# Splitting the second layer's expert routing of a batch into two planned threads, with two buffers for the normed rows

## The chip, the cores and the metric

The kernel runs on one core of a Trainium2 chip. The metric is the device time of one execution in microseconds (us); less is better. The program is one launch; its five engines are TensorE (PE, matmuls and transposes), VectorE (DVE), ScalarE (ACT), GpSimd (POOL, which here also issues the indirect DMAs), and SyncE (SP, which issues most other DMAs). Each works through its own queue in order.

## The reference

Four layers, each an attention block and then a feed-forward block, work on `x` of 4 batches x 512 tokens x 128 numbers; a context of 154 tokens is used by the cross attentions. The change lies in the feed-forward block of the second layer (`L1_ffn`), a mixture of 8 experts with a fixed capacity. What it computes, cut:

```python
S = Bb * Tt                              # 2048 tokens
C = int(CAP_FACTOR * S / E)              # 320 places per expert
logits = xf @ gate_w + gate_b            # xf: the layer-normed x
probs = jax.nn.softmax(logits, axis=1)
topk_p, topk_i = jax.lax.top_k(probs, 2)
topk_pn = topk_p / jnp.sum(topk_p, axis=1, keepdims=True)
mask = jnp.zeros((S, E), bool).at[rows[:, None], topk_i].set(True)
rank = jnp.cumsum(mask.astype(jnp.int32), axis=0)       # over all tokens, in order
slot = jnp.where(mask & (rank <= C), rank - 1, C)
...
xin = x_pad[idx]                         # the rows of each expert's tokens
h = jax.nn.relu(jnp.einsum('ecd,edh->ech', xin, w1) + b1[:, None, :])
out = jnp.einsum('ech,ehd->ecd', h, w2) + b2[:, None, :]
```

A token's rank at an expert counts the tokens of earlier batches too, so batch b's ranks need the masks of batches 0 to b. An expert can only be computed when the rows of all batches are in place.

## The kernel before

Tokens lie on the 128 partitions, four tiles of 128 to a batch. `xs[b]` holds a batch's `x` in SBUF throughout. Layers one and two are run by one call of `run(units, threads)`, a planner that writes out the order of every engine's instructions by hand. A *unit* is a quarter of a batch's attention (four of the sixteen heads): scores (`L906` in the second layer), row maxima (`L912`), their transpose (`L678`, copied to `nmT` at `L680`), the scores again with the maxima subtracted (`L927`, `L933`; the last 26 context tokens at `L945`, `L951`), exponentials on ACT (`L937`, `L954`), sums (`L779`, `L786`, kept by `L972`/`L974`), and products with the values (`L980`, `L987`, copied out at `L992`). There are 32 units, and they are the frame.

Everything else is a *thread*: a Python generator that stops at each `yield` with a text such as `"P.3 V1.3"`, the cost in us that the planner is to assume on PE (P), DVE (V), ACT (A), GpSimd (G) or DMA (D) for the next step. A thread is given with its total of PE work, the unit at which it may start, the unit by which it is due, and the threads that must be over before it starts. The planner keeps an estimated clock of each engine and puts steps of the threads into the gaps of the units, by due time, if the engine would be free. The engines then follow that order; only the semaphore waits between them are found by the framework. So the cost texts and due times decide what stands behind what in each queue. They do not change what an instruction costs.

The threads of batch b in the second layer are:

- `l1_in(b)`: norm of `xs[b]` into `xi`, its transpose, and the values.
- `qk64`: queries (`L1083`, copied by ACT at `L1086`) and keys (`L1098`, `L1103`) of a unit.
- `l1_end(b)`: reciprocals of the sums on DVE (`L1427`), their spread over partitions (`L1433`), the division (`L1440`), the output projection (`L1445`, added at `L1449`), and the bias on POOL (`L1451`).
- `l1_to(b)`: the routing. Norm: `bn_stats` and `bn_aggr` on DVE (`L240`, `L241`), `rstd` on POOL (`L268`, `L269`), the application `xr` (`L260`, on POOL, for the last batch on DVE); transpose (`L308`, copied by ACT at `L314`) and logits (`L401`, `L406`); softmax (`L1463` to `L1470`, its exponential on ACT at `L1465`); two rounds of `top2` (`L351` to `L358`, `L1475`); the sum of the two best `den` and the mask (`L1479` to `L1482`); ranks (`ranks`: running counts on DVE at `L1157`, matmuls at `L1155` and `L1158`); limits (`L1486`, `L1489`); and for each of the two choices the picks (`L1164` to `L1504`, eleven instructions) and four indirect DMAs on POOL that scatter the rows `xr` to the experts' places (`L1175`), each followed by a tiny memset.

`l1_to(b)` starts when `l1_end(b)` and `l1_to(b - 1)` are over. Its tile `xr` has one buffer, so `xr` of a batch can be written only after the scatters of the batch before have read theirs:

```python
xn = yield from norm2(rt, "xr", xs[b], fast=b == B - 1)
```

After `run`, POOL loads the experts' biases (`L1531`), SP loads expert weights (`L1536`, `L1538`) and, once all scatters have landed, the gathered rows of each expert (`L1541`); the experts' matmuls follow on PE, and then the layers three and four. A further thread, `turned_weights`, prepares weights of later layers in the meantime and ends with eight large DMAs from SP that clear a table (`L149`).

Of the kernel before, what the change touches and what calls it, by code (L numbers as in the profile page):

```python
# [13 lines left out]
F32 = mybir.dt.float32  # L14
# [8 lines left out]
B, T, D = 4, 512, 128  # L23
NQ = T // 128
# [4 lines left out]
E = 8  # L29
# [12 lines left out]
def tile_kernel(ctx: ExitStack, tc: tile.TileContext, a: dict, out: bass.AP):  # L42
    nc = tc.nc

    const = ctx.enter_context(tc.tile_pool(name="const", bufs=1))
    small = ctx.enter_context(tc.tile_pool(name="small", bufs=4))
# [7 lines left out]
    def p_a():  # L54
        return psA.tile([128, 512], F32, tag="a", name="pa")

    def over(v, shape):

        return v.unsqueeze(1).to_broadcast(shape)


    xs = [const.tile([128, NQ, D], F32, name=f"x{b}") for b in range(B)]
# [181 lines left out]
    def norm2(pool, tag, x, bufs=1, fast=False):  # L244

        mv = yield from moments2(x)
        yield "G1.3"
        r = inv_std(mv[:, :, 1])
        y = yield from applied2(pool, tag, x, mv, r, bufs, fast)
        return y  # L250
# [90 lines left out]
        )  # L341
    ctxp.close()

    def top2(l, both=True):


        sh = [128, NQ, E]

        def largest(v):
            m = small.tile([128, NQ], F32, tag="tk_m", name="tk_m")  # L350
            nc.vector.tensor_reduce(m, v, AX.X, ALU.max)  # L351
            q = small.tile(sh, F32, tag="tk_q", name="tk_q", bufs=2)
            nc.vector.tensor_tensor(q, v, m.unsqueeze(2).to_broadcast(sh), ALU.is_equal)
            nc.vector.tensor_mul(q, q, io8)
            f = small.tile([128, NQ], F32, tag="tk_f", name="tk_f")
            nc.vector.tensor_reduce(f, q, AX.X, ALU.min)
            oh = small.tile(sh, F32, tag="tk_oh", name="tk_oh", bufs=2)
            nc.vector.tensor_tensor(oh, io8, f.unsqueeze(2).to_broadcast(sh), ALU.is_equal)  # L358
            return oh, m

        oh1, m1 = largest(l)
        if not both:
            return oh1, m1
        l2 = small.tile(sh, F32, tag="tk_l2", name="tk_l2", bufs=2)
        nc.vector.scalar_tensor_tensor(l2, oh1, -3e38, l, ALU.mult, ALU.add)
        oh2, m2 = largest(l2)
        return oh1, m1, oh2, m2
# [829 lines left out]
    rt = rtctx.enter_context(tc.tile_pool(name="rt", bufs=1))  # L1197
    sg = sgctx.enter_context(tc.tile_pool(name="stage", bufs=1))
    with tc.tile_pool(name="w1", bufs=1) as w:
# [25 lines left out]
        for k, cy in ((1, D), (2, C)):  # L1225
            p = f"L2_xattn_a{k}_"
            m = mh[k] = {}
# [151 lines left out]
        units, threads = [], []  # L1379
        for b in range(B):  # L1380
# [3 lines left out]
            for t in range(4):  # L1384
                n = 4 * b + t
# [35 lines left out]
        def l1_end(b):  # L1421

            oT, rs = L1[b]["oT"], L1[b]["sums"]
            for i in range(NQ):
                yield f"V.9 @{0.1 + 0.15 * i}"
                qs = slice(i * 128, (i + 1) * 128)
                nc.vector.reciprocal(rs[:, qs], rs[:, qs])  # L1427
            for t in range(4):
                yield f"P.9 V1.3* @{0.8 + 0.15 * t}"
                rb = psS.tile([128, 2, 512], F32, tag="s", name="rb")  # L1430
                for r in range(4):
                    rows, h = slice(32 * r, 32 * r + 32), 64 * (r % 2)
                    nc.tensor.matmul(  # L1433
                        rb[h : h + 64, r // 2, :],
                        ident[rows, 32 * r + t : 32 * r + t + 1].to_broadcast([32, 64]),
                        rs[rows],
                        start=True,
                        stop=True,
                    )
                nc.vector.tensor_mul(oT[t], oT[t], rb)  # L1440
            for i in range(NQ):
                yield f"P1.8 V.3 @{1.5 + 0.1 * i}"
                py = p_a()[:, :128]
                for t in range(8):
                    nc.tensor.matmul(  # L1445
                        py, oT[t // 2][:, t % 2, i * 128 : (i + 1) * 128], wo1[:, t, :],
                        start=t == 0, stop=t == 7,
                    )
                nc.vector.tensor_add(xs[b][:, i, :], xs[b][:, i, :], py)  # L1449
            yield "G1.3"  # L1450
            nc.gpsimd.tensor_add(xs[b], xs[b], over(bc["L1_xattn_bo"], [128, NQ, D]))  # L1451

        def l1_to(b):

            sh = [128, NQ, E]
            xn = yield from norm2(rt, "xr", xs[b], fast=b == B - 1)
            yield "P.45 A.6"
            xT = to_sbuf(wk, transposed(xn), tag="xeT", bufs=1)
            yield "P.6 V.2"
            l = logits(xT, gw1, bc["L1_ffn_gate_b"])  # L1460
            yield "V.6 A.3"
            nm = small.tile([128, NQ], F32, tag="sm_m", name="sm_m")
            nc.vector.tensor_reduce(nm, l, AX.X, ALU.max)  # L1463
            nc.vector.tensor_sub(l, l, nm.unsqueeze(2).to_broadcast(sh))
            nc.scalar.activation(l, l, AF.Exp)  # L1465
            yield "V.9"
            sm = small.tile([128, NQ], F32, tag="sm_s", name="sm_s")
            nc.vector.tensor_reduce(sm, l, AX.X, ALU.add)
            nc.vector.reciprocal(sm, sm)
            nc.vector.tensor_mul(l, l, sm.unsqueeze(2).to_broadcast(sh))  # L1470
            yield "V1.1"
            oh1, m1 = top2(l, both=False)
            yield "V1.3"
            l2 = small.tile(sh, F32, tag="tk_l2", name="tk_l2", bufs=2)
            nc.vector.scalar_tensor_tensor(l2, oh1, -3e38, l, ALU.mult, ALU.add)  # L1475
            oh2, m2 = top2(l2, both=False)
            yield "V.8"
            den = small.tile([128, NQ], F32, tag="den", name="den")
            nc.vector.tensor_add(den, m1, m2)  # L1479
            nc.vector.reciprocal(den, den)  # L1480
            mask = small.tile(sh, F32, tag="mask", name="mask", bufs=2)
            nc.vector.tensor_add(mask, oh1, oh2)  # L1482
            yield "P.3 V1.3"
            pr = ranks(before, mask, b, b * NQ)
            keep = small.tile(sh, F32, tag="keep", name="keep", bufs=2)
            nc.vector.tensor_scalar(keep, pr, float(CAP), None, ALU.is_le)  # L1486

            slot = small.tile(sh, F32, tag="slot", name="slot", bufs=2)
            nc.vector.scalar_tensor_tensor(slot, pr, float(CAP), iocap, ALU.min, ALU.add)  # L1489
            for k, (oh, m) in enumerate(((oh1, m1), (oh2, m2))):  # L1490
                yield "V1.4"
                at, kept = picked(oh, slot), picked(oh, keep)
                wt = wts[b, k] = const.tile([128, NQ], F32, name=f"wt{b}{k}")
                nc.vector.tensor_mul(wt, m, den)
                nc.vector.tensor_mul(wt, wt, kept)
                ig = idxs[b, k] = const.tile([128, NQ], I32, name=f"ig{b}{k}")
                nc.vector.tensor_copy(ig, at)

                sp = spare[:, k, b, :]
                nc.vector.tensor_sub(at, at, sp)  # L1500
                nc.vector.tensor_mul(at, at, kept)
                nc.vector.tensor_add(at, at, sp)
                io = small.tile([128, NQ], I32, tag="io", name="io", bufs=4)
                nc.vector.tensor_copy(io, at)  # L1504
                for i in range(NQ):
                    yield "G1.3"
                    scatter("x1", xin1, io[:, i : i + 1], xn[:, i, :])

                    nc.gpsimd.memset(small.tile([128, 1], F32, tag="gap", name="gap", bufs=2), 0.0)

        for b in range(B):
            n = 4 * B + 4 * b
            threads.append([l1_in(b), 2.75, n - 5, n - 2])
            for t in range(4):
                units.append(unit64(wk, b, t, L1[b]))
                threads.append(
                    [qk64(L1[b], t, lambda b=b: L1[b]["q"], lambda b=b: L1[b]["k"]), 2.5, n + t - 2, n + t - 1.3]
                )
            threads.append([l1_end(b), 10.8, n + 4.7, n + 6.4])
            after = [len(threads) - 1] + ([last] if b else [])  # L1520
            last = len(threads)
            threads.append([l1_to(b), 1.35, n + 4.7, n + 9, *after])
        threads.append([turned_weights(), 9.3, 1, 24])
        run(units, threads)
        ctx1.close()
# [3 lines left out]
    with tc.tile_pool(name="m1", bufs=1) as mw:  # L1529
# [4 lines left out]
        for e in range(E):  # L1534
# [18 lines left out]
            for c2 in range(2):  # L1553
                ph = psS.tile([128, 2, 512], F32, tag="s", name="ph")
                for k in range(2):
                    c = 2 * c2 + k
# [18 lines left out]
            n = CAP - 256  # L1575
# [9 lines left out]
    with ExitStack() as stage:  # L1585
# [567 lines left out]
        units, threads = [], []  # L2153
        n_in, n_end = {1: 4.05, 2: 2.25, 3: 1.35}, {1: 14.85, 2: 14.85, 3: 9.6}
        n = 0
        for st, data, K, kind, t_in, t_end in (
# [4 lines left out]
            for b in range(B):  # L2161
                first = st == 1 and b == 0
                after = [1] if st == 1 and b == 1 else []
# [14 lines left out]
                after = [ended] if st == 3 and b else []  # L2178
                ended = len(threads)
                threads.append([t_end(b), n_end[st], n + 0.7, n + (4.7 if st < 3 else 3.8), *after])  # L2180
                if st == 3:
                    after = [len(threads) - 1] + ([last] if 0 < b < B - 1 else [])
# [38 lines left out]
```

## Time and profile before

| | |
|---|---|
| median of 3 runs | 1949.18 us (1948.55 to 1952.56) |
| the profiled execution | 1941.78 us |
| its span, first to last instruction | 1940.0 us |
| mean granted PE clock | 0.927 of full |
| PE busy | 1636.1 us, 84% of the span, 13025 matmuls |
| DVE busy | 996.6 us, 51%, 2518 instructions |
| ACT busy | 590.7 us, 30%, 925 instructions |
| POOL busy | 585.4 us, 30%, 833 instructions |
| `xin<-xr` scatters of the second layer (`L1175`) | 32, 430.2 to 619.6 us, median 962 ns each |
| `L1427` reciprocals | 16, median 918 ns |

The times in the profile are those of one execution, counted from its first instruction. A line of a timeline gives start, length, engine, line of the kernel, operation, written and read tile, shape and number of instructions; in the bracket, how long the engine stood idle before it and what ended that. A line with several instructions is a run of equal ones. Ends of matmuls are modelled, so those of neighbours can overlap. A window gives each engine's busy time in a stretch and the granted PE clock, where 1.00 is the full speed. The second layer's routing and the end of its attention lie between about 385 and 621 us.

### The profile page before, as it was taken

The page shows a single profiled execution, that of the slowest core. Times are in us where ns is not written, and L with a number is a line of the kernel's source. Part 1 is how long each engine was busy: PE and PEld are TensorE (multiplying, and loading weights), DVE is VectorE, ACT ScalarE, POOL GpSimd, SP SyncE. Part 2 cuts the span into 40 slices and gives each one's busy share as a digit, 9 for nine tenths or more (in the row PEclk, how much of TensorE's full clock was granted, in tenths as well). Part 3 has the DMA queues.
Part 4 walks back from the last instruction along what each step waited for, and adds up shares of the span by engine and source line. Part 5 has one row for each costly group of instructions (what it writes and reads, how often), then busy time and mean ns, then how long its engine had stood idle before and what let it go on. Part 6 is the DMA issues. An engine that isn't in the chain of part 4 may idle for free. (4 is left out here: it accounts for less than half of the span.)

```text
span 1940.0 us, 31600 instructions
## 1 busy us (share of the span) xinstructions
PE 1636.1 (84%) x13025; PEld 792.1 (41%) x13025; DVE 996.6 (51%) x2518; ACT 590.7 (30%) x925; POOL 585.4 (30%) x833
## 2 busy tenths in 40 slices
PE   3999999989892948999999989999999998985574
PEld 1444444434341612333333334343444444443364
DVE  3566544453443346565655544655444565656433
ACT  0333332232210113444444434233334433320011
POOL 4122202021114025233523222403323334333464
PEclk9999999999995979999999999999999998997587
DMA  8111000056002300000000000000000000020044
GB/s 163 31 61 53 14 17 6 17 94 118 12 1 68 106 12 12 12 1 12 12 1 12 1 1 12 13 1 1 1 2 1 1 1 7 1 99 6 22 141 139
DMA packets 82344, 62.34 MB, mean 32 GB/s; under 512 B 25265, under 2 KB 72441, under 8 KB 82201
## 3 DMA queue, kind: packets, MB, share of 16 engines
q1 hardware_dynamic: 67892, 39.17, 8.3%
q0 software_dynamic: 6496, 17.98, 3.1%
q10 hardware_dynamic: 7813, 3.17, 0.6%
q8 instruction: 103, 1.69, 0.4%
q14 instruction: 40, 0.33, 0.1%
HBM read 38.14 MB, written 22.72 MB: 31 GB/s over the span
## 5 line engine op out<-in xcount | busy, mean ns | idle before, releaser
L707 ACT ACTIVATE P<-ST 128x1024 f32<-128x1024 f32 (+3 forms) x320 | 270.2, 893 | 449.2 <-PE ST L699 249.6
L613 DVE TENSOR_REDUCE nm<-S 128x2 f32<-128x1024 f32 (+3 forms) x256 | 249.8, 1017 | 153.7 <-PE S L609 77.9
L691 PE MATMUL ST<-qT,kTs 32*128 32x512 f32 (+3 forms) x1024 | 165.9, 567 | 13.4 <-DVE nm L613 10.5
L599 PE MATMUL S<-kTs,qT 32*128 32x512 f32 (+3 forms) x1024 | 160.6, 566 | 11.9 <-ACT P L707 8.1
L717 POOL TENSOR_SCALAR_AFFINE_SELECT D<-P 128x512 f32<-128x512 f32 x64 | 40.7, 637 | 253.0 <-ACT P L707 252.9
L638 DVE TENSOR_REDUCE nm<-S 128x4 f32<-128x616 f32 x128 | 96.0, 793 | 26.7 <-PE S L628 26.6
L717 POOL TENSOR_SCALAR_AFFINE_SELECT P<-P 128x512 f32<-128x512 f32 x64 | 40.9, 638 | 217.0 <-ACT P L707 217.0
L691 PEld LDWEIGHTS ST<-qT,kTs 32*128 32x128 f32 x1024 | 59.4, 187 | 100.3 <-issue 44.2
L599 PEld LDWEIGHTS S<-kTs,qT 32*128 32x128 f32 x1024 | 54.3, 186 | 106.8 <-issue 52.5
L779 PE MATMUL pa<-P,tcol 128*32 128x512 f32 x768 | 97.3, 609 | 0.0
L759 PE MATMUL pa<-P,Vs 128*32 128x256 f32 (+3 forms) x896 | 74.4, 430 | 3.0 <-POOL P L717 2.1
L680 DVE COPY nmT<-ptb 128x512 bf16<-128x512 bf16 x48 | 20.2, 420 | 95.5 <-PE ptb L678 95.5
L844 ACT COPY oT<-pa 128x512 f32<-128x512 f32 x64 | 37.7, 589 | 99.0 <-PE pa L769 94.5
L912 DVE TENSOR_REDUCE nm<-S 128x4 f32<-128x616 f32 x64 | 48.1, 793 | 34.9 <-PE S L906 34.9
L628 PE MATMUL S<-kTc,qT 32*128 32x154 f32 x1024 | 54.7, 319 | 8.6 <-ACT kTc L1103 4.4
L1086 ACT ACTIVATE qT<-pa 128x512 f32<-128x512 f32 x80 | 48.3, 604 | 36.5 <-PE pa L1083 36.1
L260 POOL TENSOR_SCALAR xi<-x,mv,rstd 128x128 f32<-128x128 f32 x72 | 56.7, 799 | 1.8
L1821 DVE SCALAR_TENSOR_TENSOR x<-pa,gate,x 128x128 f32<-128x128 f32 x128 | 44.5, 350 | 24.5 <-PE pa L1813 20.5
L1175 POOL DMA_INDIRECT xin<-xr,io x32 | 31.4, 981 | 80.7 <-DVE pk L1164 40.9
L937 ACT ACTIVATE P<-ST 128x1024 f32<-128x1024 f32 x32 | 31.0, 1021 | 79.3 <-PE ST L933 79.3
L268 POOL TENSOR_SCALAR rstd<-mv 128x4 f32<-128x4 f32 (+1 forms) x46 | 9.0, 197 | 147.0 <-DVE mv L241 145.0
L1190 POOL DMA_INDIRECT yg<-y1d,ig x32 | 31.2, 974 | 70.2 <-DMA y1d<-y 60.1
(447 smaller groups left out, 3144.4 us busy)
## 6 DMA issues: line engine op xcount, KB each, us to landing
xin<-zero SPq DMA_DIRECT2D x8, 1040.0 KB
r<-in_L_ffn_w_dram SPq DMA_DIRECT2D x16, 256.0 KB
w3d<-wt SPq DMA_DIRECT2D x8, 512.0 KB
ew<-in_L_ffn_w_dram SPq DMA_DIRECT2D x16, 256.0 KB
ww<-w3d SPq DMA_DIRECT2D x4, 1024.0 KB
w_L_xattn_a_li_w<-in_L_xattn_a_li_w_dram SPq DMA_DIRECT2D x6, 256.0 KB
xin<-zero ACTq DMA_DIRECT2D x5, 256.0 KB
x<-in_x_dram SPq DMA_DIRECT2D x4, 256.0 KB
```

The source lines that it names most:

```text
L260: eng.tensor_scalar(y[:, i, :], x[:, i, :], mv[:, i, 0:1], r[:, i : i + 1], ALU.subtract, ALU.mult)
L599: nc.tensor.matmul(S2[r // 2][:, r % 2, :kv], q[32 * r : 32 * r + K, qs], k[32 * r : 32 * r + K, :kv], start=True, stop=kind != "causal",)
L613: nc.vector.tensor_reduce(nm[:, qi, 2 * rp : 2 * rp + 2], S[:, :, :kv], AX.X, ALU.max, negate=True)
L628: nc.tensor.matmul(S2[r // 2][:, r % 2, u, :KC], q[32 * r : 32 * r + K, qs], k[32 * r : 32 * r + K, :KC], start=True, stop=True,)
L638: nc.vector.tensor_reduce(nm[:, 2 * j : 2 * j + 2, 2 * rp : 2 * rp + 2].rearrange("p u r -> p r u"), S[:, :, :, :KC], AX.X, ALU.max, negat ...
L691: nc.tensor.matmul(S2[r // 2][:, r % 2, lo:], k[32 * r : 32 * r + K, ks], q[32 * r : 32 * r + K, lo:], start=True, stop=st["row"],)
L707: nc.scalar.activation(P[:, 2 * rp : 2 * rp + 2, lo:], S[:, :, lo:], AF.Exp)
L717: nc.gpsimd.affine_select(out=o, in_=d, pattern=[[0, 4], [-sg, 128]], compare_op=ALU.is_gt if kind == "upper" else ALU.is_ge, fill=0.0, ba ...
L759: nc.tensor.matmul(po[32 * r : 32 * r + 32, lo:hi], V[:, c, 4 * t + r, :], src[:, r, :], start=c == order[0] and n == 0, stop=c == order[- ...
L779: nc.tensor.matmul(ps[32 * r : 32 * r + 32], tcol[:, t, :], P[c][:, r, :], start=c == order[0], stop=c == order[-1] and "VB" not in st,)
L912: nc.vector.tensor_reduce(nm[:, 2 * j : 2 * j + 2, 2 * i : 2 * i + 2].rearrange("p u r -> p r u"), S[:, :, :, :KC], AX.X, ALU.max, negate= ...
L1086: nc.scalar.mul(q, pq, scale)
```

## The change

`l1_to(b)` becomes two threads. `l1_chosen(b)` has the norm, the logits, the softmax, the two rounds of `top2`, the mask and `den`; it starts when `l1_end(b)` is over, whatever the routing of the batch before. `l1_to(b)` keeps the ranks, the picks and the scatters, and starts when `l1_chosen(b)` and `l1_to(b - 1)` are over. What the first hands to the second lies in `chosen[b]`, in tiles of the pool `rt` with two buffers each: `xr`, the two one-hot choices and the mask; `top2` gets an argument for the tile that it writes. The PE work of 1.35 is divided into 1.05 and 0.3, the first part is due at unit n + 8.4 instead of n + 9, and the step of 0.8 us of DVE that held `den` and the mask becomes two of 0.4, the mask first. The instructions and their number stay the same.

```diff
-    def top2(l, both=True):
+    def top2(l, both=True, into=None):
...
-            oh = small.tile(sh, F32, tag="tk_oh", name="tk_oh", bufs=2)
+            oh = into
+            if oh is None:
+                oh = small.tile(sh, F32, tag="tk_oh", name="tk_oh", bufs=2)
...
-        def l1_to(b):
+        def l1_chosen(b):
 
             sh = [128, NQ, E]
-            xn = yield from norm2(rt, "xr", xs[b], fast=b == B - 1)
+            chosen[b] = c = {}
+            xn = c["xn"] = yield from norm2(rt, "xr", xs[b], 2, fast=b == B - 1)
+            for n in ("oh1", "oh2", "mask"):
+                c[n] = rt.tile(sh, F32, tag=n, name=n, bufs=2)
...
-            oh1, m1 = top2(l, both=False)
+            oh1, m1 = top2(l, both=False, into=c["oh1"])
...
-            oh2, m2 = top2(l2, both=False)
-            yield "V.8"
-            den = small.tile([128, NQ], F32, tag="den", name="den")
+            oh2, m2 = top2(l2, both=False, into=c["oh2"])
+            yield "V.4"
+            nc.vector.tensor_add(c["mask"], oh1, oh2)
+            yield "V.4"
+            den = c["den"] = small.tile([128, NQ], F32, tag="den", name="den")
             nc.vector.tensor_add(den, m1, m2)
             nc.vector.reciprocal(den, den)
-            mask = small.tile(sh, F32, tag="mask", name="mask", bufs=2)
-            nc.vector.tensor_add(mask, oh1, oh2)
+            c["m"] = m1, m2
+
+        def l1_to(b):
+
+            sh = [128, NQ, E]
+            c = chosen[b]
+            xn, oh1, oh2, mask, den = (c[n] for n in ("xn", "oh1", "oh2", "mask", "den"))
+            m1, m2 = c["m"]
             yield "P.3 V1.3"
             pr = ranks(before, mask, b, b * NQ)
...
             threads.append([l1_end(b), 10.8, n + 4.7, n + 6.4])
+            ended = len(threads) - 1
+            threads.append([l1_chosen(b), 1.05, n + 4.7, n + 8.4, ended])
             after = [len(threads) - 1] + ([last] if b else [])
             last = len(threads)
-            threads.append([l1_to(b), 1.35, n + 4.7, n + 9, *after])
+            threads.append([l1_to(b), 0.3, n + 4.7, n + 9, *after])
```

## The prediction

> **What bounds the kernel now.** The profiled execution took 1941.78 us and spans 1940.0; the runs have a median of 1949.18, so I work in differences and take them off the median. 0.2% (3.9 us) is about what a measurement of this kernel can tell from no change. The page comes first: TensorE (PE) is busy 84% of the span, so the second layer matters only where PE waits. The windows over that layer show where: PE is busy 37.64 of 40 us in 440 to 480, but 33.56 in 400 to 440, 33.78 in 480 to 520, and 24.09 of 64 in 560 to 624. I then read the timeline of those three places by engine. PE at the first two, which are batches 0 and 1:
>
> ```profile
> 419.68 1.06 PE L786 MATMUL pa<-PB,tcol 26*32 26x512 f32 x8
> 426.53 0.60 PE L1155 MATMUL pa<-mask,tri 128*128 128x32 f32 x2 [5.78 <-DVE mask L1482]
> 427.03 0.64 PE L1158 MATMUL pa<-before,ones 128*128 128x32 f32 x2
> 427.60 3.79 PE L927 MATMUL ST<-qT,kTc 64*128 64x512 f32 x8
> ...
> 506.09 1.06 PE L786 MATMUL pa<-PB,tcol 26*32 26x512 f32 x8
> 512.93 0.61 PE L1155 MATMUL pa<-mask,tri 128*128 128x32 f32 x2 [5.78 <-DVE mask L1482]
> 514.01 3.46 PE L927 MATMUL ST<-qT,kTc 64*128 64x512 f32 x8
> ```
>
> The first number is the start, the second the length, the bracket the idle time and who ended it. In both batches PE stands 5.78 us before the ranks matmul, which needs the mask of the chosen experts; the attention matmuls behind it (L927) wait in PE's queue. VectorE (DVE) at the same place shows why the mask is late:
>
> ```profile
> 417.22 0.19 DVE L406 TENSOR_TENSOR logit<-pa,bc_L_ffn_gate_b 128x32 f32<-128x32 f32 x1 [4.50 <-PE pa L401]
> 418.79 0.42 DVE L680 COPY nmT<-ptb 128x512 bf16<-128x512 bf16 x1 [1.39 <-PE ptb L678]
> 419.13 1.50 DVE L912 TENSOR_REDUCE nm<-S 128x4 f32<-128x616 f32 x2
> 420.81 0.69 DVE L972 COPY ssum<-pa 128x512 f32<-128x512 f32 x1 [0.18 <-PE pa L786]
> 421.42 0.94 DVE L1427 RECIPROCAL ssum<-ssum 128x128 f32<-128x128 f32 x1
> 422.28 0.13 DVE L1463 TENSOR_REDUCE sm_m<-logit 128x4 f32<-128x32 f32 x1
> ...
> 426.41 0.77 DVE L1157 TENSOR_TENSOR before<-before,mask 128x8 f32<-128x8 f32 x4
> ```
>
> The softmax and top two (L1463 to the mask) stand behind L680 to L1427, and DVE idles 4.50 us ahead of the logits. The third place is the end of the layer: GpSimd (POOL), then DVE.
>
> ```profile
> 586.53 1.27 POOL L1451 TENSOR_TENSOR x<-x,bc_L_xattn_bo 128x512 f32<-128x512 f32 x1
> ...
> 595.59 0.96 POOL L1175 DMA_INDIRECT xin<-xr,io  x1 [0.19 <-issue]
> 596.55 0.12 POOL L1509 MEMSET gap<- 128x1 f32 x1
> 596.76 0.20 POOL L268 TENSOR_SCALAR rstd<-mv 128x4 f32<-128x4 f32 x1
> ```
>
> ```profile
> 585.91 1.92 DVE L1501 TENSOR_TENSOR pk_r<-pk_r 128x4 f32<-128x4 f32 x1
> ...
> 589.65 0.18 DVE L241 BATCH_NORM_AGGREGATE mv<-st 128x2 f32<-128x6 f32 x1
> 598.13 1.11 DVE L260 TENSOR_SCALAR xr<-x,mv,rstd 128x128 f32<-128x128 f32 x4 [8.30 <-POOL rstd L269]
> 602.42 0.19 DVE L406 TENSOR_TENSOR logit<-pa,bc_L_ffn_gate_b 128x32 f32<-128x32 f32 x1 [3.17 <-PE pa L401]
> ```
>
> Batch 3's norm has its moments at 589.83, but its `rstd` stands behind batch 2's eight scatters on POOL and starts at 596.76. Everything after hangs on it: batch 3's scatters (610.62 to 620.60), the load of the experts' rows (622.15), PE again at 624.36. All later work needs those experts, so what is won here arrives at the end.
>
> **Part 1, batches 0 and 1.** The instruction counts are unchanged; in the changed order the logits matmul (L401) comes right after the products L980/L987, ahead of L945, and softmax, top two, mask and `den` all stand ahead of L680 on DVE. Batch 0: L987 ends at 412.53, so L401 starts there instead of at 416.12. DVE took the logits 1.10 after L401 began, so 413.63. From the logits to the end of `den` takes 4.45 by batch 3's undisturbed chain (602.42 to about 606.87), so 418.08. One reciprocal L1427 (0.94) that stood before the logits now follows, so L680 starts at 418.94 instead of 418.79: the group is hidden in the 4.50 us that DVE idled, all but 0.15. Behind it L912, L972 and the second L1427 run as before, 0.15 later, and L1157 starts at about 422.4 instead of 426.41: 4.0 earlier. PE's L1158 waits for L1157, so PE resumes 4.0 earlier. Batch 1 has the same rows 86.4 us later (L401 502.53, L1157 512.82) and the same 4.0. Sum 8.0. The exponential (L1465, 0.23) now stands ahead of L954 on ScalarE (ACT) and behind L992, which ended at 413.67 while it is wanted at 414.3: covered by 0.6. If that cover went, each us later would delay L680 and, behind it, the maxima and PE by as much.
>
> What is late next there? DVE goes from L1157 through the picks, two L1427 and L912 without a gap, so it shifts by 4.0 too. The stall that remains on PE is about 2 us instead of 5.78. In the windows the granted clock fell to 0.50 during both long stalls, and L927 took 3.79 and 3.46 after them against 1.99 elsewhere (L927 at 404.66), 3.3 us in all. But the clock also fell after shorter stalls: 2.24 us (before L1433 at 441.92) and 1.89 us (before L1098 at 529.77), both in this layer. A stall of 2 us is at that edge, so this term lies between 0 and 3.3; I take 0.5, near the rows of 1.89 and 2.24, which are the nearest in length. The Trainium skill (TensorE: Matmul & The Clock Gate, Part 1) says that the clock halves after an idle window of about 3.4 us that runs freely; by it a 2 us stall would leave the clock full and the term would be the whole 3.3. The two short stalls here speak against that, since they halved it.
>
> **Part 2, the end of the layer.** The new order on POOL is: the bias load L1531, L1451, two scatters, batch 3's `rstd`, then batch 2's other six. On DVE: picks of batch 2's first choice, batch 3's moments, `xr`, logits, and only then the picks of its second choice. PE ends its last L1445 at 583.86 as before, since the ranks' short wait (0.71) moves one L1445 group later but stays. L1531 ran 584.42 to 585.10; L1451 follows to 586.5 (before: 587.80). It meets the first picks: in the row above, L1501 lasted 1.92 instead of 0.16 and ended with L1451, so I let one op be held to 586.5. Then the indices are out at 587.3 and the moments end at 588.9. Two scatters of 1.27 from 587.5 end at 589.9, `rstd` 590.1 to 591.4, `xr` from 591.45 instead of 598.13: 6.7 won. The logits follow 4.29 later as now; then the second picks stand ahead of batch 3's softmax, eleven ops in 1.87 (582.31 to 584.18). Net 4.8. Scatters 5 to 8 of batch 2 then run until about 603, before batch 3's first indices near 606, so POOL is free. The second buffer for `xr` is what lets batch 3's rows be written while batch 2's scatters still read theirs; that costs no instruction. If L1451 holds nobody, the net is 5.8; if it holds two ops, 3.8.
>
> **Sum.** 4.0 + 4.0 + 4.8 + 0.5 = 13.3 us off 1949.2: **1936**.
>
> **The rivals.**
> (a) *The clock stays full* after the short stalls, and nothing downstream takes it back: +2.8, so 1933. For: a 1.41 us gap before L1445 at 576.44 did not halve it. Against: the 1.89 and 2.24 rows. Chance 0.2. This is where the rule of the Trainium skill named above leads (TensorE: Matmul & The Clock Gate, Part 1).
> (b) *Batch 0's gain is lost to the next wait.* There PE waits 2.24 us for ACT's L992, which starts at 440.85 though its product was ready at 437.5, while clears from SP (eight of 1040 KB, issued 417.95 to 453) run. If that moment is fixed by the clears rather than by the order of work, 4.0 of the sum and the clock term go: 1940.4. Against: batch 1 has a like wait (L954 at 528.63, product ready at 525.16) without clears, which moves with its scatters. Chance 0.15.
> (c) *The end gains nothing*: if the moments of batch 3 come out late, `rstd` stays near 596.8 and the second picks add 1.87: the sum becomes 8.5 − 1.9 = 6.6, so 1942.6. POOL's order speaks against it. Chance 0.05.
> (d) *Slower*: the softmax group now blocks L680. It waits for ACT's exponential, which stands behind L992; L992 was 3.35 us late in batch 1's first unit (440.85). If it is late by x in batches 0 and 1, PE gets its nmT x − 0.6 later, twice. The change is slower once 2(x − 0.6) exceeds 12.8, so from x = 7.0; at x = 9.2 the time would be 1953.6. No ACT row here shows such a delay where no scatters run. Chance 0.04.
> (e) *The change does nothing*, because the moved waits end with something else: 1949. The stalls name the mask and `rstd` directly, so 0.04.
>
> My forecast has the remaining 0.52. Range: (a) with a free end is 13.3 + 2.8 + 1.0 = 17.1, so 1932, and 1 more for the spread of the runs; (b) reaches 1940.4 and (c) 1942.6. I give 1931 to 1943; (d), (e) and odd ends are the 2 in 10 left out. Faster by over 0.2%: 0.91; within: 0.05; slower: 0.04.
>
> **What would show it.** In the changed profile: PE's idle before L1155 or L1158 near 2 us, not 5.78, in two places; the softmax ending before L680; `rstd` of batch 3 between scatters two and three of batch 2, about 6.5 us earlier after PE's last L1445 than now (12.9); batch 3's first scatter some 4.8 us earlier after that L1445 than 26.8. Wrong would be: an idle of PE at L933 for nmT, or a later `xr`.

## The result, and the profile after

The changed kernel takes 1934.6 us (median; 1923.3 to 1941.9) against 1950.2 (1945.5 to 1960.6) for the kernel before on the same chip: a ratio of 0.9915, with a 95% interval of 0.9892 to 0.9938. That is 15.6 us faster by the medians; 13.3 were forecast, and the forecast of 1936.0 lies 1.4 us above the median.

The two profiled executions do not show this in their totals (1941.78 us before, 1941.94 after): the first lies below all nine runs of its kernel, the second is the longest of its nine. So the reading is by stretches. Two serve for all that follows. **S1** runs from batch 0's L788 (L786 before), the last matmul ahead of its ranks, to the end of the last output projection (L1447; L1445 before). **S2** runs from there to the experts' first matmul. S1 fell from 164.2 to 151.7 us, S2 from 40.5 to 36.9: 16.1 us together. The profiled execution of the changed kernel had come to S1 5.9 us later than the other (425.56 against 419.68), with nothing changed up to there, reached the experts 10.2 us earlier (614.18 against 624.36), and lost all but 0.7 of these again between 670 and 885 us, where TensorE ran at half clock for longer than the other (34.1 us instead of 27.3 from 670 on, 6.8 instead of 3.4 from 769 on) and in two places where the other did not (837.2 to 844.1 and 857.7 to 861.1). Line numbers from 361 on are 2 or more higher than before.

TensorE in batches 0 and 1, in the timeline after:

```profile
426.56 0.41 PE L1157 MATMUL pa<-mask,tri 128*128 128x32 f32 x2
428.72 0.41 PE L1160 MATMUL pa<-before,ones 128*128 128x32 f32 x2 [1.75 <-DVE before L1159]
428.96 1.10 PE L1085 MATMUL pa<-xnT,w_L_xattn_Wq 128*128 128x512 f32 x2
430.00 1.99 PE L929 MATMUL ST<-qT,kTc 64*128 64x512 f32 x8
...
508.61 0.41 PE L1160 MATMUL pa<-before,ones 128*128 128x32 f32 x2 [1.76 <-DVE before L1159]
508.85 1.39 PE L1085 MATMUL pa<-xnT,w_L_xattn_Wq 128*128 128x512 f32 x2
510.17 3.35 PE L929 MATMUL ST<-qT,kTc 64*128 64x512 f32 x8
```

The mask no longer ends a wait: L1157 starts at once, in batch 1 too (506.44). What is left, 1.75 and 1.76 us of 5.78, is a wait for the running counts of L1159. After it L929 takes 1.99 us in batch 0 (3.79 before) but 3.35 in batch 1 (3.46 before): one of two equal waits still halves the granted clock. VectorE's timeline says why the counts come when they do:

```profile
423.63 0.19 DVE L1483 TENSOR_TENSOR mask<-oh,oh 128x32 f32<-128x32 f32 x1
...
427.30 0.94 DVE L1429 RECIPROCAL ssum<-ssum 128x128 f32<-128x128 f32 x1
428.16 0.70 DVE L1159 TENSOR_TENSOR before<-before,mask 128x8 f32<-128x8 f32 x4
```

The mask now stands ahead of L682 (424.86), and L682, the maxima, a copy and two reciprocals lie between it and the additions that need it. At the end of the layer, GpSimd and then VectorE, each by its timeline:

```profile
578.55 1.28 POOL L1453 TENSOR_TENSOR x<-x,bc_L_xattn_bo 128x512 f32<-128x512 f32 x1
582.05 1.07 POOL L1177 DMA_INDIRECT xin<-xr,io  x1 [2.22 <-issue]
...
584.62 0.19 POOL L268 TENSOR_SCALAR rstd<-mv 128x4 f32<-128x4 f32 x1
```

```profile
578.17 1.70 DVE L1507 TENSOR_TENSOR wt<-tk_m,den 128x4 f32<-128x4 f32 x1
...
581.12 0.17 DVE L1517 CAST io<-pk_r 128x4 int32<-128x4 f32 x1 [0.39 <-DVE pk_r L1515]
...
585.97 1.29 DVE L260 TENSOR_SCALAR xr<-x,mv,rstd 128x128 f32<-128x128 f32 x4 [3.09 <-POOL rstd L269]
```

Batch 3's `rstd` stands after two scatters, not eight. After the last L1447 (its end, 577.28) `xr` comes at 8.7 us, not 14.3; batch 3's first scatter at 23.0, not 26.8.

### The profile page after: what moved, and what is told of

Same layout as the page of the kernel before. It is cut to its first block, busy times and chain, and to the rows that moved or that the text cites. A ratio compares the mean times of both kernels' runs of the same rounds, so it can differ in the third digit from the quotient of the medians.

```text
span 1940.1 us, 31593 instructions
## 1 busy us (share of the span) xinstructions
PE 1642.8 (85%) x13025; PEld 793.9 (41%) x13025; DVE 995.7 (51%) x2518; ACT 590.9 (30%) x925; POOL 583.7 (30%) x833
## 5 line engine op out<-in xcount | busy, mean ns | idle before, releaser
L719 POOL TENSOR_SCALAR_AFFINE_SELECT D<-P 128x512 f32<-128x512 f32 x64 | 40.5, 635 | 263.0 <-ACT P L709 262.9
L682 DVE COPY nmT<-ptb 128x512 bf16<-128x512 bf16 x48 | 20.0, 417 | 93.0 <-PE ptb L680 93.0
L1837 DVE SCALAR_TENSOR_TENSOR x<-pa,gate,x 128x128 f32<-128x128 f32 x128 | 44.5, 350 | 24.4 <-PE pa L1829 20.5
L660 DVE SCALAR_TENSOR_TENSOR qT<-pa,sel,qT 128x512 f32<-128x512 f32 x32 | 24.0, 751 | 54.4 <-PE pa L655 54.2
L1177 POOL DMA_INDIRECT xin<-xr,io x32 | 31.5, 983 | 67.7 <-issue 36.7
```

Source lines behind the costliest of these rows:

```text
L719: nc.gpsimd.affine_select(out=o, in_=d, pattern=[[0, 4], [-sg, 128]], compare_op=ALU.is_gt if kind == "upper" else ALU.is_ge, fill=0.0, ba ...
```

## The experiments

All in one table first. "Waits" is TensorE's idle time in S1, in gaps over 0.5 us; "half clock" is the time in S1 at a granted clock of half; the ratio is to the kernel before on the same chip, with its 95% interval.

| run | S1 | S2 | waits | half clock | ratio |
|---|---|---|---|---|---|
| before (first profile) | 164.2 | 40.5 | 19.7 | 20.5 | |
| changed (first profile) | 151.7 | 36.9 | 10.5 | 6.8 | 0.9915 (0.9892 to 0.9938) |
| e1 first part only | 147.2 | 42.7 | 7.5 | 3.4 | 0.9956 (0.9940 to 0.9972) |
| e2 second part only | 159.8 | 36.7 | 14.4 | 23.9 | 0.9961 (0.9942 to 0.9979) |
| e3 additions early | 144.3 | 36.7 | 4.2 | 3.4 | 0.9901 (0.9876 to 0.9927) |
| e4 end's order | 148.3 | 32.7 | 6.7 | 6.8 | 0.9897 (0.9864 to 0.9930) |
| e5 combined | 155.7 | 30.6 | 11.6 | 17.1 | 0.9870 (0.9848 to 0.9892) |
| e6 changed again | 154.6 | 36.6 | 11.5 | 10.2 | 0.9913 (0.9890 to 0.9937) |
| e7 before again | 171.6 | 40.5 | 22.2 | 34.1 | |
| e8 due time alone | 166.7* | 40.5 | 18.5 | 30.7 | 0.9980 (0.9968 to 0.9992) |
| e9 no scatters in batch 0 | 151.0 | 36.5 | 8.1 | 10.2 | |
| e10 changed, beside e9 | 151.7 | 36.9 | 10.5 | 6.8 | |
| e11 end alone | 156.0 | 30.7 | 11.1 | 17.1 | 0.9875 (0.9846 to 0.9904) |
| e12 additions again | 153.4 | 36.5 | 10.0 | 13.7 | 0.9902 (0.9878 to 0.9925) |

e1 to e4 ran on one chip, e5 to e8 on another, e9 to e12 on a third. (*) In e8 the ranks stand earlier, so its S1 is worked out: from one attention unit earlier it took 183.3 us, and 188.2 in e7, so 171.6 − 4.9 = 166.7. Its waits and half clock are those of the longer stretch, over which e7 has 22.2 and 34.1.

**e1: the first part only.** The first thread waits for the routing of the batch before.

```diff
-            threads.append([l1_chosen(b), 1.05, n + 4.7, n + 8.4, ended])
+            threads.append([l1_chosen(b), 1.05, n + 4.7, n + 8.4, ended] + ([last] if b else []))
```

> The two threads stay, but the first one of a batch also waits for the routing of the batch before, as the old single thread did. TensorE's order is then that of the changed kernel; only the end of the layer falls back: all sixteen picks' operations of batch 2 and its eight scatters stand ahead of batch 3's rstd. Stretch S1 runs from the matmul on the 26-row tile ahead of batch 0's ranks matmul to the end of the last output projection: 164.2 us before, 151.7 changed. Stretch S2 runs from there to the experts' first matmul: 40.5 before, 36.9 changed. Theory (two separate parts): S1 149 to 154, S2 40.5 within 0.5; time 12 us below the kernel before. Rival (one part needs the other, since the norm's second buffer or the earlier picks free something in batches 0 and 1): S1 above 156, or S2 below 39.

Measured: S1 147.2, S2 42.7, ratio 0.9956 (8.5 us below before). S1 is the first part's, as the theory has it, and is even below its span. On this chip TensorE waited for ScalarE only ahead of L403 (1.03 us, as in every run), not for the late copies of batches 0 and 1 that e6 and e9 are about. The time fell by 8.5 us where 12 were expected. S2 missed the expectation by 2.2: the changed order has the ranks of batch 2 one output group later, so the first of its scatters starts 4.8 us after the last projection instead of 1.6, and with all eight ahead `rstd` ends at 16.3 instead of 14.2. So the first part alone makes the end slower, and the second part makes up for it first: against e1 it is worth 5.8 us (42.7 to 36.9), of which 3.6 are left against before.

**e2: the second part only.**

```diff
-            threads.append([l1_chosen(b), 1.05, n + 4.7, n + 8.4, ended])
+            threads.append([l1_chosen(b), 1.05, n + 4.7, n + 9, ended])
```

> The changed kernel with the first thread due at unit n + 9, as the old thread was, not n + 8.4. In batches 0 and 1 VectorE's softmax and top two fall back behind L680 to the second L1427; the end of the layer keeps the changed order. Theory (two separate parts): TensorE waits about 5.8 us again ahead of the ranks in both batches, S1 162 to 166, S2 36.9 within 0.5; time 3.6 us below the kernel before. Rival (the split alone, without the due time, brings batches 0 and 1 forward): S1 near 152.

Measured: waits of 5.65 and 5.64 us ahead of the ranks, S1 159.8, S2 36.7, ratio 0.9961 (7.5 us). The split alone does not bring batches 0 and 1 forward; the rival falls. S1 is 2.2 below the expected span; here too ScalarE is not late. Between e2 and e1, on the same chip and with the first part the only difference in batches 0 and 1, S1 is 12.5 us apart, as in the first two profiles (164.2 − 151.7). The two gains by time, 8.5 and 7.5 us, add up to 16.0, near the 15.6 of the whole change.

**e3: the additions to the running counts right behind the mask.**

```diff
             nc.vector.tensor_add(c["mask"], oh1, oh2)
+            for n in range(b * NQ, b * NQ + NQ):
+                nc.vector.tensor_add(before[:, n + 1, :], before[:, n, :], c["mask"][:, n - b * NQ, :])
...
-            pr = ranks(before, mask, b, b * NQ)
+            pr = p_a()[:, : NQ * E].rearrange("p (i e) -> p i e", e=E)
+            nc.tensor.matmul(pr, tri, mask, start=True, stop=False)
+            nc.tensor.matmul(pr, ones, before[:, b * NQ : b * NQ + NQ, :], start=False, stop=True)
```

> The changed kernel, with the four additions of the mask to the running counts taken out of the ranks and put right behind the mask on VectorE; the order of every other engine stays. In the changed kernel they stand behind the second reciprocal, and TensorE waits 1.75 us for them in batches 0 and 1. Theory (the wait that is left is these additions' place): the wait falls below 0.3 us in both, nothing else takes it, S1 falls by 3.5 for the waits and by up to 2 more where the clock no longer halves: 146 to 149; time 3.5 to 5.5 below the changed kernel, 17 to 21 below the kernel before. Rival (the next wait takes the place, the attention's exponentials on ScalarE or nmT, which comes 0.75 later): S1 151 to 153.

Measured: S1 144.3, 3.0 and 4.0 below e1 and e4 on the same chip; ratio 0.9901. TensorE's timeline shows that half of the wait went, not all:

```profile
427.14 1.13 PE L1085 MATMUL pa<-xnT,w_L_xattn_Wq 128*128 128x512 f32 x2 [0.90 <-DVE ssum L974]
428.20 1.99 PE L929 MATMUL ST<-qT,kTc 64*128 64x512 f32 x8
```

L1085 needs the PSUM buffer `pa` that L974 copies out, and that copy stands behind the maxima: 0.90 us in both batches, where "below 0.3, and nothing else takes it" was expected. But a wait of 0.90 no longer halved the clock in either batch.

**e4: another order at the end.** Batch 3's norm is a thread of its own, and batch 2's picks and scatters wait for it.

```diff
+        def l1_normed(b):
+            chosen[b] = {"xn": (yield from norm2(rt, "xr", xs[b], 2, fast=b == B - 1))}
...
+            threads.append([l1_normed(b), 0.0, n + 4.7, n + 8.4, ended])
+            if b == B - 1:
+                held = len(threads) - 1
+                last = len(threads)
+                threads.append([l1_put(b - 1), 0.0, n + 0.7, n + 5, held, ranked])
```

(`l1_put` has the picks and scatters of `l1_to`, both picks ahead of the scatters.)

> The changed kernel, with another order at the end of the layer only: batch 3's moments, rstd and xr ahead of batch 2's picks and of all its eight scatters, and both picks ahead of batch 3's logits. TensorE's order stays. In the changed kernel two scatters and the first picks, one of them held for 1.70 us, stand ahead of rstd. Theory (what is late there is rstd behind picks and scatters): moments end 4.4 us after the last L1447, rstd 5.8, xr starts 5.9 after it instead of 8.7; the softmax begins 4.0 earlier because the second picks now fill the wait for the logits; batch 3's first scatter comes 3.7 earlier and S2 is 33.2. Rival (GpSimd is then the bound: eight scatters of batch 2 end no earlier than 597.5 in the profiled execution): batch 3's first scatter within 1 us of the changed kernel's, S2 36 to 37.

Measured: S2 32.7, 4.0 below e3 on the same chip, which has the changed kernel's end; ratio 0.9897. `rstd` ends 5.7 us after the last L1447, `xr` starts at 5.7, the softmax is 4.5 earlier. GpSimd's timeline, and VectorE's:

```profile
575.66 0.19 POOL L268 TENSOR_SCALAR rstd<-mv 128x4 f32<-128x4 f32 x1 [1.82 <-DVE mv L241]
...
580.18 1.10 POOL L1177 DMA_INDIRECT xin<-xr,io  x1 [3.21 <-DVE pk L1166]
```

```profile
577.00 1.11 DVE L260 TENSOR_SCALAR xr<-x,mv,rstd 128x128 f32<-128x128 f32 x4 [1.44 <-POOL rstd L269]
...
581.57 0.18 DVE L408 TENSOR_TENSOR logit<-pa,bc_L_ffn_gate_b 128x32 f32<-128x32 f32 x1
```

The logits follow VectorE's picks without an idle gap, and `rstd` waits for moments instead of scatters. From 580.18 on GpSimd issues all sixteen scatters without a gap, one each 1.27 us: it is the bound now, but it starts earlier, so the rival (no gain) falls.

**e5: both edits, and batch 3's bias row added to x at the start of its output stage.**

```diff
             oT, rs = L1[b]["oT"], L1[b]["sums"]
+            if b == B - 1:
+                yield "G1.3"
+                nc.gpsimd.tensor_add(xs[b], xs[b], over(bc["L1_xattn_bo"], [128, NQ, D]))
```

> Both edits of the two runs before together, the additions behind the mask and the new order at the end, and one more: batch 3's bias row is added to x at the start of its output stage, not after the last projection, so that the moments need not wait for GpSimd's L1453 and nothing holds VectorE there. The parts theory: S1 as with the additions alone, 143 to 147; xr starts 3.5 us after the last L1447 instead of 5.7, all sixteen scatters, which follow each other without a gap, start 2.2 earlier, S2 30.5. S1 and S2 together 175, against 181.0 with either edit alone; time 7 to 11 us below the changed kernel. Rival (the two edits share a gain, or the bias in its earlier place holds VectorE in batch 3's last unit): S1 and S2 together 179 or more.

Measured: ratio 0.9870, the lowest of all. S2 is 30.6 and `xr` starts at 3.4, as expected. S1 is 155.7, far above the 143 to 147 expected; the changed kernel on this chip (e6) has 154.6. So the rival came true. Two things make the difference. One is waits for ScalarE (0.87, 1.88 and 3.25 us) that the chip of e3 and e4 did not have, and clock windows after them. The other is the early bias row itself, by TensorE's timeline and then VectorE's:

```profile
560.93 6.30 PE L1438 MATMUL rb<-ssum,ident 32*64 32x512 f32 x32 [1.14 <-DVE sm_m L1476]
```

```profile
559.94 0.94 DVE L1432 RECIPROCAL ssum<-ssum 128x128 f32<-128x128 f32 x1
560.79 0.13 DVE L1476 TENSOR_REDUCE sm_m<-logit 128x4 f32<-128x32 f32 x1
```

L1438 does not read `sm_m`; it reads the sums, and the last of their four reciprocals now stands behind the logits, 6.9 us after the last unit's L788 instead of 4.3 as in the kernels without the early row. From that L788 to the end of the last projection it is 24.1 us here and 24.7 in e11, which also has the early row, against 21.7 to 22.8 in the twelve others. So the row does not hold VectorE, as the rival had it, but its step in the plan costs batch 3's last unit some 2 us.

**e6 and e7: the changed kernel and the kernel before, once more.** No edit.

> The changed kernel once more, beside the others. Theory: S1 146 to 152 and S2 36.7 again; TensorE waits 1.75 us ahead of the second ranks matmul in both batches, and whether the clock halves after it depends on whether 1.7 us or more of the wait fall into one 3.41 us window of the clock's grid. ScalarE's 3.3 us of lateness (L994 and L956), which the first two profiles showed while scatters ran, and which none of the last four profiles has, is not the program's: absent here too. Rival: the lateness belongs to the program's order and is there again.

> The kernel before once more, for its profile. Theory: waits of 5.8 us ahead of the ranks in batches 0 and 1, S2 40.5; without ScalarE's lateness (2.24 and 1.89 us of TensorE's waits) S1 is 158 to 162 rather than 164.2. Rival (the lateness belongs to the program): S1 near 164 with both waits.

Measured in e6: S1 154.6, S2 36.6, waits of 1.75 and 1.75 us ahead of L1160; in e7: 171.6, 40.5, waits of 5.78 and 5.79. The change gains 17.0 + 3.9 = 20.9 us in this pair. The expectation on ScalarE fell: its lateness was there again, and cost TensorE 1.93 and 2.05 us in e6, 3.10 and 3.46 in e7. It goes with the chip, since e1 and e2 had none of it with these orders of instructions.

**e8: one due time, no second thread.**

```diff
-            threads.append([l1_to(b), 1.35, n + 4.7, n + 9, *after])
+            threads.append([l1_to(b), 1.35, n + 4.7, n + 8.4, *after])
```

> The kernel before with one number changed: its single routing thread is due at unit n + 8.4 instead of n + 9. The planner then puts the ranks matmuls right behind the logits matmul on TensorE, ahead of the attention's L945, and all of softmax, picks ahead of L680 on VectorE. Theory (two threads are needed, because the ranks must stay late on TensorE while the mask comes early): TensorE waits for the mask from the logits on, 4.5 us or more ahead of the ranks in batches 0 and 1, S1 162 or above, no gain, time within 5 us of the kernel before or slower. Rival (the due time alone is the gain): S1 near 150.

Measured: a wait of 4.57 and 4.56 us for the mask ahead of the ranks, S1 166.7, ratio 0.9980. It gains some 4 us (1.6 to 6.3) of the changed kernel's 17. The mask did come forward: it ends 14.9 us after that earlier unit's L786, against 23.3 in e7 and 14.8 in the changed kernel. But the ranks came forward on TensorE with it and wait for it there. What the split adds is that the ranks stay late.

**e9 and e10: what makes ScalarE late.** e9 leaves out batch 0's eight scatters, with the tiny memset behind each; e10 is the changed kernel beside it.

```diff
+                    if b == 0:
+                        continue
                     scatter("x1", xin1, io[:, i : i + 1], xn[:, i, :])
```

> The changed kernel without batch 0's eight scatters (its rows are left out of the experts' input); every other instruction stays in its place. TensorE's results reached ScalarE and VectorE late in batches 0 and 1 in six of the ten profiles so far, always while eight scatters ran; TensorE then waited 1.9 to 3.5 us for ScalarE 14 to 24 us after the ranks. Theory (the scatters make it): no such wait in batch 0, a wait of 1 to 3.5 us still in batch 1, if this chip shows the lateness at all, which the run beside this one tells. Rival (the clears from SyncE make it, which run in batch 0 only): the wait in batch 0 stays.

> The changed kernel on the same chip, as the other half of the run without batch 0's scatters. Theory: if the lateness shows on this chip, in both batches, 1 to 3.5 us each. A wait of 1.75 us ahead of the second ranks matmul in both batches; the clock halves after it only if 1.7 us of it lie in one window of 3.41 us. Rival: none of this run's own.

Measured: ScalarE's copies of the attention output and of the probabilities in batch 0, in e9 and then in e10:

```profile
433.89 1.01 ACT L994 COPY oT<-po 128x1024 f32<-128x1024 f32 x1 [2.60 <-PE po L989]
436.11 0.60 ACT L956 ACTIVATE PB<-SB 128x512 f32<-128x512 f32 x1 [1.21 <-PE SB L953]
```

```profile
436.91 1.01 ACT L994 COPY oT<-po 128x1024 f32<-128x1024 f32 x1 [4.02 <-PE rb L1435]
441.32 0.60 ACT L956 ACTIVATE PB<-SB 128x512 f32<-128x512 f32 x1 [3.40 <-PE pa L1100]
```

In e9 L994 starts when its product L989 ends (433.83), in e10 1.5 us after it (L989 ended at 435.42); L956 starts 0.1 us and 3.7 us after its product. The named releasers of e10 are later matmuls that these copies do not read. TensorE's wait of 1.88 us in batch 0 is gone in e9, while batch 1, with its scatters, still has one of 1.46. So the scatters (with their memsets) make the lateness, not the clears, which run in both; the rival falls. How a scatter keeps a finished product from ScalarE was not found.

**e11 and e12: the combined kernel taken apart again.** e11 has the end's order and the early bias row without the additions; e12 is e3's kernel on this chip.

> The combined kernel without the additions behind the mask: the new order at the end and batch 3's bias row added early. Theory (the end's gain stands by itself, on any chip): S2 30.6, as in the combined kernel; xr 3.4 us after the last L1447; TensorE waits 1.75 us again ahead of the second ranks matmul. Time 5 to 9 us below the changed kernel's ratio of 0.9913, so 0.987 to 0.989. Rival (the end's gain came with the additions): S2 above 32.

> The kernel with only the additions behind the mask once more, on another chip. On the first one S1 was 144.3, with no lateness of ScalarE; in the combined kernel, on a chip with lateness, S1 was 155.7 against the changed kernel's 154.6. Theory (where the scatters make ScalarE late, TensorE, coming sooner, waits for it the longer, and the additions' gain is eaten): on a chip with lateness S1 is within 2 us of 151.7 to 154.6 and the ratio within 0.002 of 0.9913; on a chip without, S1 144 to 145 and ratio near 0.990. Rival (the combined kernel lost it through its early bias row): S1 148 to 150 with lateness there.

Measured: e11 has S2 30.7, `xr` at 3.4, ratio 0.9875, so S2's gain does not need the additions. But its S1 is 156.0, 4.3 above e10's, and e11 differs from e4 by the early bias row alone: that row takes 2.1 us off S2 (32.7 to 30.7) and adds 2.0 to batch 3's last unit (22.8 to 24.7). What is left of the end's gain is the 4.0 of e4, measured on that chip. e12 has S1 153.4 and 0.9902, where the changed kernel has 151.7 (e10) and 0.9913 (e6, on another chip): the additions' gain is eaten on this chip, without any early bias row, by waits for ScalarE of 0.76, 1.90 and 3.11 us. TensorE, let go sooner, waits there instead. The combined kernel (0.9870) and e11 cannot be told apart. On its chip the combined kernel beats the changed one: all five runs of e5 (1922.2 to 1931.3) lie below all six of e6 (1931.4 to 1945.0), by 7.0 us in the median. For e11 this is not shown: the one run of the changed kernel on its chip (e10) took 1932.3, e11 1931.5 in the median.

## Why the prediction was right

**Part 1, the waits: right to 0.1 us.** 4.0 us less in each batch was forecast. The waits fell from 5.78 to 1.75 and 1.76, so by 4.03 and 4.02. e2 gave them back by the due time alone, and S1 with them. The order forecast for VectorE came out too: L682 starts 0.70 us before L788, 0.89 before the same matmul in the kernel before, so 0.19 later where 0.15 was forecast.

**The clock term: the step that was mis-sized.** "I take 0.5, near the rows of 1.89 and 2.24": of S1's 12.45 us in the first pair, 8.05 are the waits for the mask and 1.2 ScalarE's (2.24 + 1.89 down to 1.89 + 0.55 + 0.51), so about 3.2 are left for the clock, with half-clock time down from 20.5 to 6.8 us. But the term was worked out on L927, and there it measures 1.9: 1.80 in batch 0 (3.79 to 1.99) and 0.11 in batch 1 (3.46 to 3.35). The rest lies in other instructions, among them those of a window that the term did not count: behind batch 1's wait for ScalarE the kernel before ran at 0.50 from 530.68 to 534.09, while the changed one has a clock of 1.00 from 512.95 to the end of S1. So the likeness of 3.2 to the upper end, 3.3, is chance. The term was sized by the length of a wait, and length does not decide it. The clock changes only on a fixed grid of 3.41 us (its 46 to 70 stretches in each of the fourteen profiles all begin on one), and what counts is how much of one window TensorE is busy. In the windows of the changed kernel (time, span, then busy time and count of TensorE first; the clock is the third number from the end):

```profile
424.20:427.60 3.40, 2.76 (x24) 0.83 (x22) 3.34 (x6) 0.00 (x0) 0.00 (x0) 1.00 0.12 1
427.60:431.00 3.40, 2.28 (x10) 1.06 (x12) 2.75 (x17) 0.60 (x1) 0.00 (x0) 1.00 0.78 114
506.10:509.50 3.40, 1.64 (x10) 0.82 (x6) 2.89 (x10) 0.00 (x0) 0.00 (x0) 1.00 0.00 0
509.50:512.90 3.40, 3.40 (x10) 1.19 (x8) 2.92 (x21) 0.60 (x1) 0.89 (x1) 0.51 0.00 0
```

Batch 0's wait of 1.75 us is cut in two by the grid, leaves 2.76 and 2.28 us busy, and the clock stays full. Batch 1's 1.76 lies whole in one window, leaves 1.64 of 3.40 busy, and the next window runs at half. In the seven profiles with a wait of this length ahead of L1160 (changed, e1, e4, e6, e9, e10, e11) it halved the clock six times in batch 1 and once in batch 0. The Trainium skill (TensorE: Matmul & The Clock Gate, Part 1) has the grid of 3.41 us that runs freely, and the runs agree; its idle window of that length is not needed: half of one was enough.

**Part 2: right in kind, 1.2 us too large.** 4.8 was forecast, S2 fell by 3.6. The step is "Then the indices are out at 587.3" and the scatters after it: the prediction started the first scatter 3.6 us after the last projection, and it came at 4.8. The held operation took 1.70 us (L1507; 1.92 in the row used), as forecast; behind it came 0.39 us of idle ahead of the last cast, and 0.8 us from the cast's end (581.29) to the scatter. `rstd` and all that follows carried the 1.1 us on: forecast at 7.5 us after the last projection, ended at 8.7. The logits then came 4.5 instead of 4.29 after `xr`, and the second picks took the 1.87 that were forecast (590.55 to 592.41, the softmax starting within). e4 shows the place was the right one: with `rstd` ahead of picks and scatters S2 loses 4.0 more.

**The rivals.** (a), the clock staying full, came half true: in batch 0 of two, for 1.9 of its 3.3 us on L927. (b), batch 0's gain lost to ScalarE's L992 and fixed by SyncE's clears, is refuted by e9: the scatters make that wait, and they move with the routing. The argument against it, that batch 1 has a like wait without clears, was the right one. (c) needs a late `rstd`; it was early. (d) needs a late exponential: L1470 ran at 420.24, 0.03 us after the end of the L1469 that it reads. (e) is out by the interval.

So the sum was 13.3 where the two stretches show 16.1 in the first pair: −1.2 at the end, +2.7 in the clock, +1.2 in ScalarE's waits, which no step had counted. That the forecast lies only 1.4 us from the median is partly luck: these misses run against each other, and the kernel before had a median of 1950.2 in this comparison, 1.0 above the 1949.2 from which the sum was taken off.

## What to carry to other kernels

When a chain feeds two engines, ask which of its operations the other engine needs, and put only these early: here the mask and its four additions (the additions gained on one chip, in e3, and nothing on another, in e12), while ranks, picks and scatters may stay late. At the end of a stage, let the next batch's short serial steps (moments, `rstd`) go ahead of the last batch's bulk (picks, scatters) on every queue, since the bulk then fills the waits of the serial chain. When a step is moved across the border of two stretches, as the bias row in e5 and e11, read both: what one gained the other lost. Judge a small change by local stretches between fixed instructions: the two profiles agreed to 0.2 us in all, and two stretches had won 16.

## What the hardware showed that was not expected

**The clock follows how busy TensorE was in the window before.** Over fourteen profiles I cut the span into the windows of 3.41 us that the clock's own changes mark, leaving out the start-up. After a window at full clock in which TensorE was busy for less than 40% the next was at half in 202 of 202; for 40 to 50% in 54 of 82; for 50 to 60% in 9 of 89; for 60 to 90% in about 110 of 1370; for 90% and more in 5 of 4774. From half clock it never came back after a window under 70% busy (0 of 509), and in 329 of 422 after one of 90% or more. The ends of matmuls are modelled, so the edges are soft, and why the middle band has its 8% was not looked into. A wait of 0.9 us, as in e3, costs itself; one of 1.75 costs up to about 1.7 more, by where it falls (L1085 and L929 took 1.65 longer in batch 1 than in batch 0).

**Scatters delay what another engine has finished.** While eight indirect DMAs were issued on GpSimd, ScalarE took up some of TensorE's products 1.2 to 4.8 us late on every chip but one, and in e8 VectorE did so too (L972 at 435.73, its product ready at 432.53). On that one (e1 to e4) nothing was late, and the kernel before ran in 1933 us there against 1950 to 1954. Whether the later layers' scatters cost those 17 to 21 us in the same way was not tried.
